# A of the fourth pair of heads for the first four batches by 11 block products, placed between the two halves of U

## Chip, cores and metric

The kernel runs on one core of a Trainium2 chip. The metric is the device time of one execution in microseconds (us). The engines are PE (TensorE, matrix products; PEld is its loading of weights), DVE (VectorE), ACT (ScalarE), POOL (GpSimd) and SP (SyncE, which only issues DMAs here). Each works its own instructions in the order of the program, and waits on semaphores for the others.

## Reference

Cross-attention with 8 heads of 256, all in float32: x is 16 x 256 x 256 (batch, queries, width), c is 16 x 77 x 192.

```python
Q = (x @ Wq).reshape(B, -1, H, D).transpose(0, 2, 1, 3)
K = (c @ Wk).reshape(B, -1, H, D).transpose(0, 2, 1, 3)
V = (c @ Wv).reshape(B, -1, H, D).transpose(0, 2, 1, 3)
score = jnp.einsum('bhqd,bhkd->bhqk', Q, K) / math.sqrt(D)   # masked keys: -inf
attn = softmax(score)
ctx = jnp.einsum('bhqk,bhkd->bqhd', attn, V).reshape(B, -1, H * D)
out = ctx @ Wo + x
return layernorm(out) * gamma + beta
```

## Kernel before

The kernel folds weights. Per head, G = Wk Wq^T / 16 (192 x 256) is made once, so that the scores are x (G^T c^T); the product A = G^T c^T (256 x 77 for a head and batch) takes the place of K and Q. Likewise U = Wv Wo per head takes the place of V and the output projection. The batches go in four groups of four (GB = 4); a row tile is 128 queries, two for a batch, 32 in all.

G is kept in gA (its first 128 rows, for all 8 heads) and gB (its last 64 rows, two heads of a pair above each other); c, turned, in cA and cB in the same split. U is kept in uA and uB.

A is made in one of two ways.

- Straight: `prepare_a`, whose products into the banks pa are lines L203 (with gA) and L215 (with gB). The first group's A is made so, one pair of heads at a time (`a_of_pairs`).
- By 11 block products in place of 12: `prepare_fast`, in the manner of Strassen and Winograd. It takes one pair of heads of a group, and treats batches 0-1 and 2-3 of the group and the halves of G as 2 x 2 blocks. `products()` issues 44 matrix products (line L361) into four PSUM banks pf, a middle and an end bank for each head; ACT copies one product of each head out on the way (L370); `put_together(e)` adds a head's blocks up into A with four operations of DVE (L373). The operands are sums and differences of blocks: of G in gS (`sums_of_g`, `last_sums_of_g`) with a copy gC, of c in cT and cD (`sums_of_c`, `differences_of_c`), all made by POOL after copies of ACT. Groups 1 and 2 of four use it; t_of and cD are indexed by the group less one.

The lines of the start, in the program's order:

1. Loads. SP issues them all in one queue; a load waits for the eighth before it to land. POOL issues every second block of Wv (wvT) in its own queue.
2. Wk and Wq of a pair are turned (`turn_blk`, DVE) into kT and qT; then gB's products (phb, L1033), gA's (pgb, L1017), and A of the pair (pa). Pair 0 goes by other lines. kT lies in a room with the tag gS; after the last pair the same room is given to the sums of G.
3. Wv is turned (`turn_v`, DVE, L945).
4. U, in two halves j of two pairs each: `of_pair` into banks pu (L956), copies into uA; `rest_of_pairs` into banks pw (L970), copies into uB.
5. Scores of the first two row tiles (ps, L469), masking and maxima on DVE (`shift`, L486), exponentials on ACT (L512), weights p on POOL (`weigh`, L533), turned on DVE (`turn`, L543).
6. `prepare_last` (pr, L429 and L440), U times c for two batches (pv, L393 and L404), A of group 1 by `prepare_fast` for two pairs (pf), and so on in steps of two batches.

PSUM has eight banks, given out in turn: a tile waits until the reader of the tile eight banks before it is done. With it, the scores of row tile 2 take the banks of pf's first pair, and the scores of row tile 4 the last two banks of pf's second pair.

The order on each engine is the order of the code (`manual_schedule`).

Of the kernel before, what the change touches and what calls it, by code (L numbers as in the profile page):

```python
# [9 lines left out]
F32 = mybir.dt.float32  # L10
# [6 lines left out]
P = 128  # L17
H = 8
# [9 lines left out]
def kernel(  # L28
# [13 lines left out]
    nc = tc.nc  # L42
# [45 lines left out]
    cT = const.tile([P, 4, FAST, KX], F32, tag="cT", name="cT")  # L88
    cD = const.tile([P, FAST, KX], F32, tag="cD", name="cD")
    gC = const.tile([P, NF, P], F32, tag="gC", name="gC")  # L90

    def flat(ap):
        return ap.rearrange("p a b -> p (a b)")
# [34 lines left out]
    def half(i):  # L128
        return slice(i * LB, (i + 1) * LB)
# [99 lines left out]
        partial(nc.gpsimd.tensor_tensor, op=op) for op in (ALU.add, ALU.subtract)  # L229
    )  # L230

    def parts_of_g():
        parts = gA.rearrange("p (u e) (dc i c) -> p dc e u i c", e=2, dc=2, c=BK)
        sums = gS.rearrange("p n (u e) (i c) -> p n e u i c", e=2, c=BK)
        return [(parts, sums, e, own, other) for e, own, other in ((0, high, low), (1, low, high))]

    def sums_of_g():


        for parts, sums, e, own, other in parts_of_g():  # L240
            nc.scalar.copy(sums[own, 0, e], parts[other, 1, e])
            nc.scalar.copy(gC[own], gB[other, :, P:])
        for parts, sums, e, own, other in parts_of_g():
            s1, s2, s3 = (sums[own, n, e] for n in range(3))
            add(s1, s1, parts[own, 1, e])
            subtract(s2, s1, parts[own, 0, e])
            subtract(s3, parts[own, 0, e], parts[own, 1, e])

    def last_sums_of_g():


        for parts, sums, e, own, other in parts_of_g():
            nc.scalar.copy(sums[other, 0, e], sums[own, 1, e])
        for parts, sums, e, own, other in parts_of_g():
            subtract(sums[other, 0, e], parts[other, 0, e], sums[other, 0, e])

    def halves_of(c, lo, hi):
        groups = c[:, lo * GB : hi * GB].rearrange("p (g y b) k -> p y g (b k)", y=2, b=HB)
        return groups[:, 0], groups[:, 1]

    def sums_of_c(lo, hi):


        xs, ys = halves_of(cA, lo, hi)
        t1, t2, t3, t4 = (cT[:, n, lo - 1 : hi - 1] for n in range(4))
        subtract(t1, ys, xs)
        for own, other in ((low, high), (high, low)):
            nc.gpsimd.tensor_copy(t2[own], ys[other])
        subtract(t3, t2, ys)
        subtract(t2, t2, t1)  # L270
        for own, other in ((low, high), (high, low)):
            nc.gpsimd.tensor_copy(t4[own], t2[other])
        subtract(t4, xs, t4)

    def differences_of_c(lo, hi):
        subtract(cD[:, lo - 1 : hi - 1], *halves_of(cB, lo, hi))

    def prepare_fast(g, u):

# [19 lines left out]
            return lambda i: gA[rows, h, dc * P + i * LB : dc * P + (i + 1) * LB]  # L299

        def from_s(rows, n, h):
            return lambda i: gS[rows, n, h, half(i)]

        def from_rest(h, dc):
            return lambda i: gB[half(h % 2), h // 2, dc * P + i * LB : dc * P + (i + 1) * LB]
# [2 lines left out]
            return flat(of[rows, which])  # L308

        def t_of(rows, n):  # L310
            return cT[rows, n, g - 1]

        def middle(e):

# [13 lines left out]
        def outer(e):  # L328

            h, own = heads[e], (low, high)[e]  # L330
            return [
                ((ends[e], 0), from_g(own, h, 0), c_of(cA, own, xs)),
                ((ends[e], 1), from_s(own, 0, h), c_of(cA, own, ys)),
                ((ends[e], 2), from_g(own, h, 1), t_of(own, 3)),
                ((ends[e], 0), from_rest(h, 0), c_of(cB, own, xs)),
                ((ends[e], 1), from_rest(h, 0), c_of(cB, own, ys)),
                ((ends[e], 2), from_rest(h, 1), cD[own, g - 1]),
            ]

        def pairs():  # L340
# [442 lines left out]
    with tc.tile_pool(name="wonce", bufs=1) as wp:  # L783
# [15 lines left out]
        def load_blocks(to, blocks, queues=(nc.sync,)):  # L799
            for i in range(NM):  # L800
                queues[i % len(queues)].dma_start(to[i * BK : (i + 1) * BK], blocks[i])
# [35 lines left out]
            return parts[::-1] if a == 1 else parts  # L837

        qT_blk = [const.tile([P, 4, DI], F32, tag=f"xg{a}", name=f"qT_{a}") for a in range(NF)]
        kT_all = const.tile([P, NF, 4, DL], F32, tag="gS", name="kT_all")  # L840
        kT_blk = [kT_all[:, a] for a in range(NF)]
        qT = qT_blk[0].rearrange("p (e dc) d -> p e dc d", e=2)
        kT = kT_blk[0].rearrange("p (e dc) l -> p e dc l", e=2)
        for a in range(1, NF):
# [21 lines left out]

        def load_late():

            for a in range(NF):
                load_blocks(wvT[a], wv_blocks[a], (nc.sync, nc.gpsimd))  # L870
            for a in range(NF):
                nc.sync.dma_start(wo_of[a // 2][:, a % 2], wo_rows[a])
            load_xT(0, QT)
            load_bias(0, GB)
            load_rest()
            load_xT(QT, PT)
            load_xT(PT, GT)
            load_bias(GB, B)
# [65 lines left out]
        def turn_v(a):  # L944
            nc.vector.transpose(  # L945
                wv_turned[:, a].rearrange("p n (r m) -> p m n r", r=BK),
                wvT[a].rearrange("p m (c n) -> p m n c", n=4),
            )
# [112 lines left out]
        turn_k_last()  # L1061
        g_of(1)
        turn_c()
        load_late()
        rest_of_g()
        turn_blk(1)
        a_of_pairs(0)
        for a in range(1, NF):
            rest_of_g_of_pair(a)
            g_of_pair(a)  # L1070
            if a < NF - 1:
                turn_blk(a + 1)
            else:
                for i in range(3):
                    turn_v(i)
            a_of_pairs(a, rest_first=True)
        gS = const.tile([P, 3, H, P], F32, tag="gS", name="gS")
        sums_of_g()
        load_x(0)
        load_x(1)  # L1080
        nc.sync.dma_start(gam, gamma.partition_broadcast(P))
        nc.sync.dma_start(bet, beta.partition_broadcast(P))
        turn_v(3)

        def sum_of(u):
            t2, _, b22, b11, b12 = (u[:, q].rearrange("p n i c -> p (n i c)") for q in range(5))
# [3 lines left out]
        for j in range(NF // 2):  # L1090
            pu = two_banks("pu", j)
            for a in range(2 * j, 2 * j + 2):
                of_pair(pu, a, wv_part, wo_part)
            if j:
                transpose_x(0)
                bias_of(0, GB)
            for e, copy in enumerate((nc.scalar.copy, nc.scalar.copy if j else nc.vector.tensor_copy)):
                copy(
                    of_e(uA, e)[:, :, 2 * j : 2 * j + 2].rearrange("p n a c -> p a n c"),
                    pu[e].rearrange("p a (n c) -> p a n c", c=BK),  # L1100
                )
            if j:
                sum_of(uA)
            for e, pw in enumerate(
                rest_of_pairs(j, (2 * j, 2 * j + 1), wv_part, wo_part, "pw")
            ):
                copy = (nc.scalar.copy, nc.vector.tensor_copy)[e]
                for i in range(2):
                    for k in range(2):
                        copy(  # L1110
                            of_e(uB, e)[half(k), :, 2 * j + i],
                            pw[half(i)].rearrange("p (n c) -> p n c", c=BK),
                        )
        last_sums_of_g()
        for t in range(QT):
            scores(t)
        turn_rest()
# [291 lines left out]
```

## Time and profile before

| | |
|---|---|
| median of 3 runs | 269.1 us (268.92 to 269.33) |
| the profiled execution | 268.58 us |
| its span in the profile | 266.8 us |
| PE, PEld | 260.5 us (98%), 202.8 us (76%) |
| DVE, ACT, POOL | 212.7 us (80%), 166.9 us (63%), 191.5 us (72%) |
| granted clock of PE | 1.0 in the span's mean |

The span is the time between the first and the last instruction of the trace. Busy time is what each engine worked in it. A row of the chain gives its start, its length and what it is; "x32" counts records, and a float32 product has two. A row of a timeline gives start, busy time, engine, line, operation, output<-input with partitions x elements, and in brackets how long the engine stood idle ahead of it, and what ended that.

### The profile page before, as it was taken

Reading aid. Unit: us, or ns where it says so; the run is one execution under the profiler, and the core shown is the slowest. Engines: PE = TensorE matmul, PEld = TensorE weight load, DVE = VectorE, ACT = ScalarE, POOL = GpSimd, SP = SyncE. Lnnn points to the kernel's source line nnn. Section 1 sums busy time; section 2 is a strip of 40 time slices with the busy share of each in tenths; the row PEclk is TensorE's granted clock in tenths of the full one; section 3 lists DMA queues with packets and bytes.
Section 4 is the critical chain, followed back from the end, with each engine's and each line's share of the span. In section 5 each row is a group of like instructions: output and inputs, shape, how many; then the busy total and the mean of one; then the engine's idle time right before and its main releaser. Section 6 shows DMA issues by size and latency. Waiting matters only on the chain.

```text
span 266.8 us, 15067 instructions
## 1 busy us (share of the span) xinstructions
PE 260.5 (98%) x6330; PEld 202.8 (76%) x6330; DVE 212.7 (80%) x860; ACT 166.9 (63%) x710; POOL 191.5 (72%) x272
## 2 busy tenths in 40 slices
PE   7999999999999999999999999999999999999992
PEld 6566578948986899679967996799669957985662
DVE  0554968479893789988997969898988798799785
ACT  3253548624584689648983798467964595636772
POOL 1042098799459896899479996997699899685452
PEclk9999999999999999999999999999999999999999
DMA  6999997900240002131314012221234010100112
GB/s 188 209 206 225 335 148 160 300 18 4 63 104 5 2 6 66 58 90 37 83 43 122 5 24 65 81 85 41 54 127 132 20 44 2 44 23 25 42 43 80
DMA packets 41699, 22.73 MB, mean 85 GB/s; under 512 B 24144, under 2 KB 40608, under 8 KB 41632
## 3 DMA queue, kind: packets, MB, share of 16 engines
q1 hardware_dynamic: 41248, 20.98, 31.3%
q0 software_dynamic: 384, 0.79, 1.3%
q8 instruction: 50, 0.82, 1.3%
q14 instruction: 17, 0.14, 0.2%
HBM read 17.57 MB, written 4.19 MB: 82 GB/s over the span
## 4 chain that ended last, share of the span: by engine, by line
PE 96%; DMA 2%; DVE 1%; SPq 0%; issue 0%; DVEq 0%
PE ps L469 25%; PE pf L361 11%; PE po L622 11%; PE pv L393 10%; PE pm L622 9%; PE pv L404 6%; PE pa L203 5%; PE po L555 4%; PE pu L956 3%; PE pa L215 2%; PE pr L429 2%; PE pgb L1017 2%; DMA wq_nat<-in_L_xattn_Wq_dram 2%; PE pw L970 1%; PE pr L440 1%; PE phb L1033 1%
## 5 line engine op out<-in xcount | busy, mean ns | idle before, releaser
L512 ACT ACTIVATE s<-s,top 128x77 f32<-128x77 f32 x256 | 85.2, 346 | 24.5 <-DVE top L486 24.5
L469 PE MATMUL ps<-a,xT 128*32 128x154 f32 x2048 | 70.1, 294 | 0.0
L469 PEld LDWEIGHTS ps<-a,xT 128*32 128x32 f32 x2048 | 65.8, 110 | 2.0 <-issue 1.5
L533 POOL TENSOR_TENSOR p<-s,rden 128x512 f32<-128x512 f32 x64 | 47.7, 769 | 21.9 <-DVE rden L527 21.7
L486 DVE CUSTOM_DVE_ANT_0 s<-ps,bias 128x77 f32<-128x77 f32 x256 | 43.3, 232 | 4.6 <-PE ps L469 4.0
L512 ACT ACTIVATION_READ_ACCUMULATOR s<-s,top 128x1 f32 x224 | 41.9, 187 | 0.0
L373 DVE TENSOR_TENSOR a<-pf,a 128x154 f32<-128x154 f32 x80 | 33.9, 435 | 7.3 <-PE pf L361 4.9
L664 POOL TENSOR_TENSOR xg<-xg,m 128x256 f32<-128x256 f32 x39 | 28.8, 738 | 2.7 <-DVE xg L676 0.7
L543 DVE STREAM_TRANSPOSE pT<-p 128x640 f32<-128x640 f32 x32 | 26.3, 827 | 5.1 <-POOL p L533 5.0
L393 PE MATMUL pv<-uA,cA 128*32 128x512 f32 x256 | 29.6, 593 | 0.0
L1150 ACT COPY vw<-pv 128x512 f32<-128x512 f32 x32 | 17.1, 587 | 14.9 <-PE pv L404 14.9
L760 DVE SCALAR_TENSOR_TENSOR xg<-xg,rstd,bet 128x256 f32<-128x256 f32 x27 | 22.7, 840 | 2.6 <-ACT rstd L711 1.2
L586 POOL TENSOR_TENSOR ts<-vw 128x768 f32<-128x768 f32 x13 | 23.6, 1831 | 0.0
L486 DVE DVE_READ_ACCUMULATOR2_ANT top<- 128x1 f32 x256 | 20.9, 82 | 0.0
L393 PEld LDWEIGHTS pv<-uA,cA 128*32 128x32 f32 x256 | 8.0, 110 | 13.3 <-issue 9.8
L731 DVE SCALAR_TENSOR_TENSOR xg<-xg,mv,gam 128x256 f32<-128x256 f32 x30 | 18.0, 600 | 0.1
L361 PE MATMUL pf<-cT,gS 64*64 64x154 f32 x240 | 17.4, 290 | 0.0
L603 POOL TENSOR_TENSOR ss<-pT 128x256 f32<-128x256 f32 x13 | 9.7, 745 | 9.8 <-DVE pT L543 9.7
L404 PE MATMUL pv<-uB,cB 64*32 64x512 f32 x256 | 16.3, 596 | 0.0
L622 PE MATMUL po<-vr,pT 128*32 128x256 f32 x208 | 16.0, 379 | 0.0
L361 PEld LDWEIGHTS pf<-cT,gS 64*64 64x64 f32 x240 | 15.8, 133 | 0.0
L203 PE MATMUL pa<-cA,gA 128*32 128x308 f32 (+1 forms) x256 | 14.0, 360 | 0.0
(153 smaller groups left out, 543.1 us busy)
## 6 DMA issues: line engine op xcount, KB each, us to landing
xg<-in_x_dram SPq DMA_DIRECT2D x8, 512.0 KB, 4.4
xT<-in_x_dram SPq DMA_DIRECT2D x56, 64.0 KB, 2.7
out_dram<-xg SPq DMA_DIRECT2D x11, 256.0 KB, 2.7
wo<-in_L_xattn_Wo_dram SPq DMA_DIRECT2D x4, 512.0 KB, 7.9
wq_blk<-in_L_xattn_Wq_dram SPq DMA_DIRECT2D x12, 128.0 KB, 4.6
out_dram<-xg SPq DMA_DIRECT2D x10, 128.0 KB, 1.7
wk_blk<-in_L_xattn_Wk_dram SPq DMA_DIRECT2D x12, 96.0 KB, 4.0
wvT<-in_L_xattn_Wv_dram POOLq DMA_DIRECT2D x8, 96.0 KB, 6.3
```

Of the source, the lines that this page charges most:

```text
L203: nc.tensor.matmul(flat(o[i * BK : (i + 1) * BK]), gA[:, h, cols(dc, i)], flat(cA[:, batches, :]), start=not rest_first and n in opening, ...
L361: nc.tensor.matmul(bank[half(i), n], weight(i), moving, start=start, stop=stop,)
L373: nc.vector.tensor_tensor(out, *of, ALU.add)
L393: nc.tensor.matmul(pv[k][i * BK : (i + 1) * BK], cA[:, b, k * BK : (k + 1) * BK], uA[:, parts, :, i], start=not rest_first, stop=rest_first,)
L404: nc.tensor.matmul(pv[k][i * BK : (i + 1) * BK], cB[half(k), b, k * BK : (k + 1) * BK], uB[half(k), parts, :, i], start=rest_first, stop=n ...
L469: nc.tensor.matmul(ps[m // 2][i * BK : (i + 1) * BK, m % 2 * 2 * S2 : (m % 2 + 1) * 2 * S2], xT_of[t // PT][:, j * NM + m, dc], flat(a_of[ ...
L486: nc.vector.tensor_tensor_reduce(s[:, h], ps[a][:, k * S2 : (k + 1) * S2], bias[:, b, :], scale=-1.0, scalar=FAR, op0=ALU.add, op1=ALU.min ...
L512: nc.scalar.activation(s[:, h], s[:, h], AF.Exp, bias=top[:, one], scale=-1.0, accum_out=den[:, one] if summed_by_act(t) else None,)
L533: nc.gpsimd.tensor_tensor(part, e_mh[:, :, :, keys], rden_mh.unsqueeze(3).to_broadcast(list(part.shape)), ALU.mult,)
L543: nc.vector.transpose(pT_of[t].rearrange("p n m q -> p m n q"), p.rearrange("p m (n k) -> p m n k", k=BK),)
L622: nc.tensor.matmul(out[i * BK : (i + 1) * BK], weight[:, i], moving, start=first and n == 0, stop=final and n == len(terms) - 1,)
L664: nc.gpsimd.tensor_tensor(to, to, what, ALU.add)
```

## The change

A of the fourth pair of heads (a = 3, heads 6 and 7) of the first group is no longer made straight, right behind its G, but by `prepare_fast(0, 3)`, in the loop over the halves of U, behind the first half's products. For that:

- sums and differences of c of the first group are made right behind `turn_c`, on POOL, in the places of cT and cD that group 3 takes later (`places_of`, and `(g - 1) % FAST`);
- the sums of G are made by pairs. gS becomes one tile of 4 x 3 x 2 x 128 per partition, which holds a pair's turned Wk until that pair's G is made, and then its sums. The fourth pair's sums come first (`sums_of_g(3, 4)`, `last_sums_of_g(3, 4)`), behind its G; those of the other three come behind the first half of U;
- Wv's turns: the first goes ahead of the fourth pair's gB copies, the second behind them, the last two into the first half of U, where `transpose_x(0)` goes too;
- the copies of the first half of U out of pu and pw are all ACT's (before, DVE copied one of the two pu banks and one of the two pw banks);
- the loads of Wv and Wo are interleaved by halves.

```diff
+    gS = const.tile([P, NF, 3, 2, P], F32, tag="gS", name="gS")
...
-    def parts_of_g():
+    def parts_of_g(lo, hi):
         parts = gA.rearrange("p (u e) (dc i c) -> p dc e u i c", e=2, dc=2, c=BK)
-        sums = gS.rearrange("p n (u e) (i c) -> p n e u i c", e=2, c=BK)
-        return [(parts, sums, e, own, other) for e, own, other in ((0, high, low), (1, low, high))]
...
+        sums = gS.rearrange("p u n e (i c) -> p n e u i c", c=BK)
+        return [
+            (parts[:, :, :, lo:hi], sums[:, :, :, lo:hi], e, own, other)
+            for e, own, other in ((0, high, low), (1, low, high))
+        ]
...
+    def places_of(lo, hi):
+        return slice((lo - 1) % FAST, (hi - 2) % FAST + 1)
...
-        t1, t2, t3, t4 = (cT[:, n, lo - 1 : hi - 1] for n in range(4))
+        t1, t2, t3, t4 = (cT[:, n, places_of(lo, hi)] for n in range(4))
...
-            return cT[rows, n, g - 1]
+            return cT[rows, n, (g - 1) % FAST]
...
-            for a in range(NF):
-                load_blocks(wvT[a], wv_blocks[a], (nc.sync, nc.gpsimd))
-            for a in range(NF):
-                nc.sync.dma_start(wo_of[a // 2][:, a % 2], wo_rows[a])
+            for j in range(NF // 2):
+                for a in range(2 * j, 2 * j + 2):
+                    load_blocks(wvT[a], wv_blocks[a], (nc.sync, nc.gpsimd))
+                for a in range(2 * j, 2 * j + 2):
+                    nc.sync.dma_start(wo_of[j][:, a % 2], wo_rows[a])
...
         turn_c()
+        sums_of_c(0, 1)
+        differences_of_c(0, 1)
...
             if a < NF - 1:
                 turn_blk(a + 1)
-            else:
-                for i in range(3):
-                    turn_v(i)
-            a_of_pairs(a, rest_first=True)
-        gS = const.tile([P, 3, H, P], F32, tag="gS", name="gS")
-        sums_of_g()
+                if a == NF - 2:
+                    turn_v(0)
+                a_of_pairs(a, rest_first=True)
+        turn_v(1)
+        sums_of_g(NF - 1, NF)
+        last_sums_of_g(NF - 1, NF)
...
-        turn_v(3)
...
             if j:
-                transpose_x(0)
                 bias_of(0, GB)
-            for e, copy in enumerate((nc.scalar.copy, nc.scalar.copy if j else nc.vector.tensor_copy)):
-                copy(
+            for e in range(2):
+                nc.scalar.copy(
...
-            for e, pw in enumerate(
-                rest_of_pairs(j, (2 * j, 2 * j + 1), wv_part, wo_part, "pw")
-            ):
-                copy = (nc.scalar.copy, nc.vector.tensor_copy)[e]
+            rests = rest_of_pairs(j, (2 * j, 2 * j + 1), wv_part, wo_part, "pw")
+            if j == 0:
+                products, put_together = prepare_fast(0, NF - 1)
+                products()
+            for e, pw in enumerate(rests):
+                copy = nc.vector.tensor_copy if j and e else nc.scalar.copy
...
+            if j == 0:
+                for i in range(2, NF):
+                    turn_v(i)
+                transpose_x(0)
+                for e in range(2):
+                    put_together(e)
+                sums_of_g(0, NF - 1)
-        last_sums_of_g()
+        last_sums_of_g(0, NF - 1)
```

**POOL**, from the sums of G (gS) to the last two of them, before (nan and bias belong to the mask, uA is half of U):

```order
L245 TENSOR_TENSOR gS<-gS,gA 64x4x128
L246 TENSOR_TENSOR gS<-gS,gA 64x4x128
L247 TENSOR_TENSOR gS<-gA 64x4x128
L245 TENSOR_TENSOR gS<-gS,gA 64x4x128
L246 TENSOR_TENSOR gS<-gS,gA 64x4x128
L247 TENSOR_TENSOR gS<-gA 64x4x128
L777 TENSOR_TENSOR nan_634<-nan_634 128x4
L778 TENSOR_TENSOR nan_634<-nan_634 128x4
L779 TENSOR_TENSOR bias<-bias,nan_634 128x308
L1087 TENSOR_TENSOR uA<-uA 128x512
L1088 TENSOR_TENSOR uA<-uA 128x512
L255 TENSOR_TENSOR gS<-gA,gS 64x4x128 x2
```

POOL now, from the first sums of the three pairs on (ahead of these rows stand the fourth pair's eight, on 64x128):

```order
L249 TENSOR_TENSOR gS<-gS,gA 64x3x128
L250 TENSOR_TENSOR gS<-gS,gA 64x3x128
L251 TENSOR_TENSOR gS<-gA 64x3x128
L249 TENSOR_TENSOR gS<-gS,gA 64x3x128
L250 TENSOR_TENSOR gS<-gS,gA 64x3x128
L251 TENSOR_TENSOR gS<-gA 64x3x128
L784 TENSOR_TENSOR nan_682<-nan_682 128x4
L785 TENSOR_TENSOR nan_682<-nan_682 128x4
L786 TENSOR_TENSOR bias<-bias,nan_682 128x308
L1095 TENSOR_TENSOR uA<-uA 128x512
L1096 TENSOR_TENSOR uA<-uA 128x512
L259 TENSOR_TENSOR gS<-gA,gS 64x3x128 x2
```

The mask and U stood behind six operations on four pairs (64x4x128); now they stand behind eight on one pair and six on three pairs (64x3x128).

**ACT**, from the last copy of A to the second half of U, before (gC is the copy of gB, uA and uB are U):

```order
L1055 COPY a_256<-pa_7_1_0_489 128x4x77
L241 COPY gS<-gA 64x4x128
L242 COPY gC<-gB 64x512
L241 COPY gS<-gA 64x4x128
L242 COPY gC<-gB 64x512
L1098 COPY uA<-pu_0_536 128x2x8x32
L1110 COPY uB<-pw_0_572 64x8x32 x4
L1098 COPY uA<-pu_0_598 128x2x8x32
L1098 COPY uA<-pu_1_599 128x2x8x32
L1110 COPY uB<-pw_0_643 64x8x32 x4
```

ACT now, from the copies for the fourth pair's last sums on:

```order
L257 COPY gS<-gS 64x128 x2
L1105 COPY uA<-pu_0_514 128x2x8x32
L1105 COPY uA<-pu_1_515 128x2x8x32
L377 COPY a_265<-pf_6_0_568 128x2x77
L377 COPY a_265<-pf_7_1_570 128x2x77
L1119 COPY uB<-pw_0_550 64x8x32 x4
L1119 COPY uB<-pw_1_551 64x8x32 x4
L245 COPY gS<-gA 64x3x128
L246 COPY gC<-gB 64x384
L245 COPY gS<-gA 64x3x128
L246 COPY gC<-gB 64x384
L1105 COPY uA<-pu_0_647 128x2x8x32
```

The copies that start the sums of G (L241, now L245) stood ahead of all copies of U; those of three pairs now stand behind the first half of U, behind two copies of pf and behind eight copies of pw.

**SP**, the loads of Wv (wvT) and Wo, before:

```order
L801 DMA wvT_145<-in_L_xattn_Wv_dram 32x6x128 x2
L801 DMA wvT_146<-in_L_xattn_Wv_dram 32x6x128 x2
L801 DMA wvT_147<-in_L_xattn_Wv_dram 32x6x128 x2
L801 DMA wvT_148<-in_L_xattn_Wv_dram 32x6x128 x2
L872 DMA wo_143<-in_L_xattn_Wo_dram 128x1024 x2
L872 DMA wo_144<-in_L_xattn_Wo_dram 128x1024 x2
```

And now:

```order
L808 DMA wvT_145<-in_L_xattn_Wv_dram 32x6x128 x2
L808 DMA wvT_146<-in_L_xattn_Wv_dram 32x6x128 x2
L879 DMA wo_143<-in_L_xattn_Wo_dram 128x1024 x2
L808 DMA wvT_147<-in_L_xattn_Wv_dram 32x6x128 x2
L808 DMA wvT_148<-in_L_xattn_Wv_dram 32x6x128 x2
L879 DMA wo_144<-in_L_xattn_Wo_dram 128x1024 x2
```

Wo's first half moved ahead of the second half of Wv.

More of the change, by code (lines that the diff above doesn't have):

```diff
@@ L230, with sums_of_g @@
     )
-    def parts_of_g():
+    def parts_of_g(lo, hi):
         parts = gA.rearrange("p (u e) (dc i c) -> p dc e u i c", e=2, dc=2, c=BK)
-        sums = gS.rearrange("p n (u e) (i c) -> p n e u i c", e=2, c=BK)
-        return [(parts, sums, e, own, other) for e, own, other in ((0, high, low), (1, low, high))]
-    def sums_of_g():
-        for parts, sums, e, own, other in parts_of_g():
+        sums = gS.rearrange("p u n e (i c) -> p n e u i c", c=BK)
[3 more added lines that the diff above has]
+        ]
+    def sums_of_g(lo, hi):
+        for parts, sums, e, own, other in parts_of_g(lo, hi):
             nc.scalar.copy(sums[own, 0, e], parts[other, 1, e])
-            nc.scalar.copy(gC[own], gB[other, :, P:])
-        for parts, sums, e, own, other in parts_of_g():
+            nc.scalar.copy(gC[own, lo:hi], gB[other, lo:hi, P:])
+        for parts, sums, e, own, other in parts_of_g(lo, hi):
             s1, s2, s3 = (sums[own, n, e] for n in range(3))
@@ L247, in sums_of_g, with last_sums_of_g @@
             subtract(s3, parts[own, 0, e], parts[own, 1, e])
-    def last_sums_of_g():
-        for parts, sums, e, own, other in parts_of_g():
+    def last_sums_of_g(lo, hi):
+        for parts, sums, e, own, other in parts_of_g(lo, hi):
             nc.scalar.copy(sums[other, 0, e], sums[own, 1, e])
-        for parts, sums, e, own, other in parts_of_g():
+        for parts, sums, e, own, other in parts_of_g(lo, hi):
             subtract(sums[other, 0, e], parts[other, 0, e], sums[other, 0, e])
@@ L275, in differences_of_c @@
     def differences_of_c(lo, hi):
-        subtract(cD[:, lo - 1 : hi - 1], *halves_of(cB, lo, hi))
+        subtract(cD[:, places_of(lo, hi)], *halves_of(cB, lo, hi))
     def prepare_fast(g, u):
@@ L301, in from_s @@
         def from_s(rows, n, h):
-            return lambda i: gS[rows, n, h, half(i)]
+            return lambda i: gS[rows, u, n, h % 2, half(i)]
         def from_rest(h, dc):
@@ L336, in outer @@
                 ((ends[e], 1), from_rest(h, 0), c_of(cB, own, ys)),
-                ((ends[e], 2), from_rest(h, 1), cD[own, g - 1]),
+                ((ends[e], 2), from_rest(h, 1), cD[own, (g - 1) % FAST]),
             ]
@@ L839 @@
         qT_blk = [const.tile([P, 4, DI], F32, tag=f"xg{a}", name=f"qT_{a}") for a in range(NF)]
-        kT_all = const.tile([P, NF, 4, DL], F32, tag="gS", name="kT_all")
-        kT_blk = [kT_all[:, a] for a in range(NF)]
+        kT_blk = [gS[:, a].rearrange("p n e c -> p (n e c)").rearrange("p (n l) -> p n l", n=4) for a in range(NF)]
         qT = qT_blk[0].rearrange("p (e dc) d -> p e dc d", e=2)
```

## Prediction

> **What bounds the kernel now.** I read the page first, then the chain of waits between 0 and 85 us, then the timelines of POOL, ACT and DVE between 20 and 80 us, last the landing of the weight loads. The page:
>
> ```profile
> span 266.8 us, 15067 instructions
> PE 260.5 (98%) x6330; PEld 202.8 (76%) x6330; DVE 212.7 (80%) x860; ACT 166.9 (63%) x710; POOL 191.5 (72%) x272
> PE 96%; DMA 2%; DVE 1%; SPq 0%; issue 0%; DVEq 0%
> ```
>
> PE is the chain: 96% of it. After the first 7 us PE stands idle nowhere, so each microsecond of products removed is a microsecond gained, and each new wait of PE is lost for good. The place of the change, in the chain (start, us, what):
>
> ```profile
> 26.56 1.73 PE pgb L1017 x32
> 28.29 1.04 PE pa L215 x16
> 29.32 2.21 PE pa L203 x32
> 31.53 3.62 PE pu L956 x64
> 35.15 1.73 PE pw L970 x32
> 36.87 3.45 PE pu L956 x64
> ...
> 52.20 3.01 PE pr L440 x32
> ...
> 60.66 5.93 PE pf L361 x176
> 66.59 4.32 PE ps L469 x128
> ...
> 74.83 4.19 PE ps L469 x128
> ```
>
> The two pa rows at 28.29 and 29.32 are A of the fourth pair, which the change takes out. The pf row is two pairs done by the 11 block products (A of batches 4 to 7), which is the row that prices what is put in. The next rows are of POOL, whose work is what can make PE wait later (start, us busy, in brackets the idle time before and what ended it):
>
> ```profile
> 17.16 4.67 POOL L801 DMA_DIRECT2D wvT<-in_L_xattn_Wv_dram  x8 [6.56 <-DMA wk_blk<-in_L_xattn_Wk_dram]
> 32.80 1.29 POOL L245 TENSOR_TENSOR gS<-gS,gA 64x512 f32<-64x512 f32 x1 [10.97 <-ACT gS L241]
> 39.31 1.26 POOL L247 TENSOR_TENSOR gS<-gA 64x512 f32<-64x512 f32 x1
> 41.34 0.20 POOL L777 TENSOR_TENSOR nan<-nan 128x4 f32<-128x4 f32 x1 [0.77 <-DVE nan L776]
> 45.16 2.63 POOL L255 TENSOR_TENSOR gS<-gA,gS 64x512 f32<-64x512 f32 x2
> 48.88 0.93 POOL L823 COPY cB<-cB 64x896 f32<-64x896 f32 x1 [1.09 <-DVE cB L822]
> 49.86 0.36 POOL L824 COPY last_rows<-cB 128x208 f32<-128x208 f32 x1
> 56.29 2.72 POOL L533 TENSOR_TENSOR p<-s,rden 128x512 f32<-128x512 f32 x4
> 58.97 1.00 POOL L276 TENSOR_TENSOR cD<-cB 128x462 f32<-128x462 f32 x1
> 60.03 0.74 POOL L603 TENSOR_TENSOR ss<-pT 128x256 f32<-128x256 f32 x1
> ```
>
> Between 32.80 and 59.97 POOL has only two gaps, 0.77 and 1.09 us, and from 48.88 none. What waits for its end is DVE:
>
> ```profile
> 27.89 6.20 DVE L945 STREAM_TRANSPOSE wv_turned<-wvT 128x768 f32<-128x768 f32 x4
> 59.05 0.85 DVE L543 STREAM_TRANSPOSE pT<-p 128x640 f32<-128x640 f32 x1 [0.49 <-POOL p L533]
> 63.83 5.46 DVE L373 TENSOR_TENSOR a<-pf,a 128x154 f32<-128x154 f32 x12
> 72.43 0.20 DVE L527 RECIPROCAL rden<-den 128x8 f32<-128x8 f32 x1 [0.62 <-ACT s L512]
> 72.55 1.80 DVE L373 TENSOR_TENSOR a<-pf,a 128x154 f32<-128x154 f32 x4
> ```
>
> p of tile 1 leaves POOL at 59.01 (56.29 + 2.72) and DVE starts on it at 59.05; from there it runs without a gap until the put-together rows at 63.83. These free the PSUM banks of pf. PE's scores of tile 2, at 66.59, take the banks of pf's first head, free after four of the twelve operations, at 63.83 + 5.46 x 4/12 = 65.65: 0.94 us to spare. Its scores of tile 4, at 74.83, take the banks of pf's last head, free at 72.55 + 1.80 = 74.35: 0.48 us to spare. So POOL's order is already within half a microsecond of PE's chain.
>
> **The change, part by part.**
>
> *Products.* Out go 1.04 + 2.21, that is 28.29 to 31.53, 3.24 us; in come 44 products, half of the pf row: 2.97 us. All of it is on the chain: -0.27 us.
>
> *U starts earlier.* pu's first product now follows pgb, at 28.29 and not 31.53. It needs the first turned Wv, the first half of Wo and the second Wv 1.73 us later. The turns take 6.20/4 = 1.55 us each; the first goes ahead of gB's copies, into DVE's idle time; the second starts at 27.89 as the first does now, and ends by 29.5, ahead of 30.0. The loads:
>
> ```profile
> L801 SPq DMA_DIRECT2D wvT<-in_L_xattn_Wv_dram x2: 602/602/602, 19.8 to 20.5; - x2
> DMA to landing us min/median/max: 6.7/6.8/6.9
> L801 POOL DMA_DIRECT2D wvT<-in_L_xattn_Wv_dram x1: 567/567/567, 21.3 to 21.3; - x1
> DMA to landing us min/median/max: 7.3/7.3/7.3
> L872 SPq DMA_DIRECT2D wo<-in_L_xattn_Wo_dram x1: 592/592/592, 23.9 to 23.9; - x1
> DMA to landing us min/median/max: 7.1/7.1/7.1
> ```
>
> SP's second-tile Wv load issued at 19.8 lands at 26.5 and the third tile's, at 20.5, at 27.4; Wo's first load takes that place now. Before, Wo landed at 31.0, 3.6 us after the 27.4 of that third tile, with three more Wv loads of SP's queue ahead of it, about 0.9 us apiece by the spacing 26.5 to 27.4; it took some 0.9 to 1.1 us itself. So 26.5 + 1.1 = 27.6 is the low end, no wait; if POOL's own queue, whose last Wv load lands at 21.3 + 7.3 = 28.6, goes wholly first, 29.7, a wait of 1.4 us. The two queues' loads land side by side, so I stay near the low end: 0.1 us.
>
> *Sums of the first group of c.* Seven small operations and a difference on POOL, put behind turn_c: today the same seven and uB's two sums lie between 50.22 (49.86 + 0.36) and 56.29, and two sums of that size take 2.63 (L255), so the seven take 3.4 us, and the difference of 154 columns under 0.74 (a row of 256). POOL's idle 6.56 us before 17.16 covers them. Cost 0; without that cover the Wv loads of POOL's queue would be late.
>
> *Sums of G for the fourth pair.* Eight operations on 128 columns, about 0.47 us each by the line through 256 and 512 columns (0.74 and 1.27), on POOL from about 29.3 (pgb's end at 28.29, then ACT's two copies of gA and one of gS) to about 33.1: idle there today (10.97). The new pf starts at 28.29 + 0.1 + 3.62 + 1.73 = 33.74: 0.6 us to spare, cost 0.
>
> *Sums of G for the other three pairs.* This is what costs. ACT prepares them, and its row now reads: two copies of the new pf, eight copies of pw (four were DVE's), then the copies for the sums.
>
> ```profile
> 32.04 0.62 ACT L241 COPY gS<-gA 64x512 f32<-64x512 f32 x1
> 36.92 1.50 ACT L1110 COPY uB<-pw 64x256 f32<-64x256 f32 x4 [1.14 <-PE pw L970]
> 45.05 0.37 ACT L819 COPY last_rows<-cA 128x208 f32<-128x208 f32 x1 [0.17 <-DVE cA L818]
> 61.66 0.29 ACT L370 COPY a<-pf 128x154 f32<-128x154 f32 x1 [0.22 <-PE pf L361]
> ```
>
> The second copy of pf ends 61.66 + 0.29 - 60.66 = 1.29 us behind pf's start, the eight take 3.00, the copy of 384 columns lies between 0.37 (208) and 0.62 (512): 0.51; POOL starts 0.14 behind it (32.04 + 0.62 to 32.80). So POOL starts 4.94 us behind pf, at 38.68, where today three of its six operations are done. One operation on 384 columns lies midway between 256 columns, 0.74, and 512, 1.27: 1.00 us. The six took 7.77 (32.80 to 40.57), now 7.77 x 1.00/1.27 = 6.12, to 44.80. The mask's three and uA's two follow, as between 41.34 and 45.16, 3.82, and the last two sums, 2.63 x 1.00/1.27 = 2.07. POOL comes to cB's copy at 38.68 + 6.12 + 3.82 + 2.07 = 50.69, and not 48.88: **1.81 us late**, both its gaps being used up.
>
> From there nothing on POOL gives way, so p of tile 1, DVE's chain behind it and the banks come 1.81 us late: the banks for tile 4 at 74.35 + 1.81 = 76.16, where PE started at 74.83. PE starts that much later: **+1.33 us** against before, the 0.27 won included. (At tile 2 the same reckoning gives 65.65 + 1.81 - 66.59 = +0.87, the first part of it.) Behind it DVE waits for PE again, and the lateness stays.
>
> The Trainium skill, GPSIMD Engine Reference, Elementwise — side-by-side cycle accounting, gives about 2.6 cycles an element at 1.2 GHz for such a two-input operation: 0.83 us for 384 columns (an estimate from that page), with which the sum would come to about -0.1 us. By that rule 512 columns would be 1.11, where this trace has 1.27: it agrees in the slope (256 to 512 columns: 2.07 ns each) but leaves out a part of 0.2 us.
>
> *Other moves.* DVE gets eight put-together operations (3.6 us) and loses four copies of pw and one of uA; they end near 41, ahead of pw's end at about 41.9, behind which the scores read them. The mask's sum on POOL comes 3.46 us later (44.80 against 41.34); the masking of tile 0 then waits for it some 1 us, which brings the banks that pr's last products want just in time. cRB is copied at 50.22 + 1.81 = 52.03, just when PE's L440 row (52.20 - 0.17) wants it: 0 to 0.1 us, and absorbed in the later wait. xg, gamma and beta load for work far behind. Cost 0.
>
> Sum: the profiled execution took 268.58 us (span 266.8 and 1.8 around it), 0.5 below the median 269.1 of the runs; 268.58 + 1.33 = 269.9, on the median's scale **270.4 us**, 0.5% slower.
>
> **Rivals.**
>
> *The cover holds.* POOL's wide operations are cheaper than midway, or ACT reaches the sums sooner, so that POOL is less than 0.31 us late (0.48 spare less the 0.17 that PE is early). It needs operations of about 0.81 us on 384 columns. Then only the products count: 269.1 - 0.27 + 0.1 = 268.9, no change to be measured; with more luck in pu's start (3.62 the first time against 3.45 the second) 268.7. For it: a page's rule, above. Against it: every POOL row of this size. This is the case that ends not slower; 20%.
>
> *Wo late.* If the loads of POOL's queue go first, pu waits up to 1.4 us, and all that follows with it: 270.4 + 1.3 = 271.7. For it: Wo lands today 0.5 us before its use. Against: the two queues are served side by side. 12%.
>
> *Lateness partly made up.* If DVE or ACT save time between 59 and 74 us, only tile 2's wait is left, or less: +0.3 to +0.9, 269.4 to 270.0. Within my forecast's own range.
>
> **How the numbers follow.** The forecast (a POOL order that comes 1 to 2.3 us late, 269.6 to 270.9) 62%, the cover holds 20%, Wo late 12%, something unseen 6%. The range reaches from the cover that holds, 268.9, to part of Wo's wait, 271.3. A measurement of this kernel can tell about 0.2%, 0.54 us, from no change. Slower: 52 of the forecast's 62, Wo's 12, 1: 65%. Same: 10 and 13 of the cover's 20, 1: 24%. Faster: 11%.
>
> **What would show it.** In the chain after: pgb followed at once by pu near 28.3, one pf row of x88 and 2.97 us near 33.7; ACT's copies of pw eight in a row; POOL's first 64x384 operation near 38.7 at 1.00 us and cB's copy near 50.7 with no idle before it; DVE's turn of p's second tile near 60.9 behind POOL; PE idle before the scores of tiles 2 and 4, released by DVE a, about 1 and 0.5 us. Wrong, if 64x384 takes 0.85 or less, if cB's copy still waits for DVE, or if PE waits at pu for Wo.

## The result: 0.7% slower, by loads and not by POOL

| | before | after |
|---|---|---|
| median of the runs | 269.1 us (268.92 to 269.34, 6 runs) | 271.17 us (270.41 to 271.58, 6 runs) |
| ratio after / before | | 1.0072, 95% interval 1.0057 to 1.0087 |
| the profiled execution, its span | 268.58 us, 266.8 us | 271.23 us, 269.2 us |

The forecast was 270.4, in a range of 268.9 to 271.3, with the sign right; the middle of that range (269.6 to 270.9) was missed. The profile after says that the sign came about in another way, and one of the prediction's own signs of being wrong is there: PE waits at pu for Wo. The page's shares of the chain, and the chain itself from the start of U on:

```profile
PE 86%; DMA 7%; SPq 4%; DVE 1%; issue 1%; DVEq 0%
```

```profile
21.45 10.73 DMA wo<-in_L_xattn_Wo_dram
32.31 1.96 PE pu L963 x32
34.27 1.73 PE pw L977 x32
36.00 2.88 PE pf L368 x88
38.88 3.45 PE pu L963 x64
42.33 1.73 PE pw L977 x32
44.06 4.33 PE ps L476 x128
...
68.59 0.14 issue
68.74 4.39 PE ps L476 x128
...
77.05 4.23 PE ps L476 x128
```

Where the chain was 96% PE, 11% of it is now loads and their issue (2% before). It leaves PE at the second load of Wo. PE's own timeline and its waits show how long it stood:

```profile
26.80 1.91 PE L1024 MATMUL pgb<-qT,gS 64*64 64x256 f32 x32
29.91 1.96 PE L963 MATMUL pu<-wo,wv_turned 64*64 64x256 f32 x32 [1.20 <-DVE wv_turned L952]
32.31 1.96 PE L963 MATMUL pu<-wo,wv_turned 64*64 64x256 f32 x32 [0.45 <-DMA wo<-in_L_xattn_Wo_dram]
```

Wo's loads, by the view of their tile (issue times at the end of the first row):

```profile
L879 SPq DMA_DIRECT2D wo<-in_L_xattn_Wo_dram x2: 592/1154/1717, 20.8 to 21.4; - x2
DMA to landing us min/median/max: 9.0/9.8/10.7
```

They were asked for 3.1 and 3.3 us sooner than before (23.9 and 24.7), and landed at 29.8 and 32.2, where they had landed at 31.0 and 32.2. DVE's turns of Wv and of x's first tiles:

```profile
24.81 1.67 DVE L952 STREAM_TRANSPOSE wv_turned<-wvT 128x768 f32<-128x768 f32 x1 [0.40 <-DMA wvT<-in_L_xattn_Wv_dram]
...
28.28 1.59 DVE L952 STREAM_TRANSPOSE wv_turned<-wvT 128x768 f32<-128x768 f32 x1
...
38.89 0.71 DVE L176 STREAM_TRANSPOSE xT<-xT 128x512 f32<-128x512 f32 x1 [2.60 <-DMA xT<-in_x_dram]
39.63 3.70 DVE L380 TENSOR_TENSOR a<-pf,a 128x154 f32<-128x154 f32 x8
...
67.45 5.45 DVE L380 TENSOR_TENSOR a<-pf,a 128x154 f32<-128x154 f32 x12
...
76.18 1.80 DVE L380 TENSOR_TENSOR a<-pf,a 128x154 f32<-128x154 f32 x4
```

The first wait is put down to DVE, whose second turn of Wv ends at 29.87 (28.28 + 1.59); but these first products read the first turn, done at 26.48, and Wo's first load, landed at 29.8. A releaser is inferred from what came last, and here two things came together. The profile of e2 (below) tells them apart: there PE starts on pu before the second turn is done, at 29.98 (28.38 + 1.60), and right behind Wo's load, issued at 20.98 and landed 8.4 us later:

```profile
29.48 1.96 PE L963 MATMUL pu<-wo,wv_turned 64*64 64x256 f32 x32 [0.66 <-DMA wo<-in_L_xattn_Wo_dram]
```

```profile
28.38 1.60 DVE L952 STREAM_TRANSPOSE wv_turned<-wvT 128x768 f32<-128x768 f32 x1
```

From the last pgb on (its start differs by 0.42 us between the two profiles, and that start is as late in a run of the kernel before that differs only behind it, b1 below), the account is:

- U's first half: 5.56 us (from pgb's end, 26.80 + 1.91 = 28.71, to 34.27) for 3.62: **+1.94**. Of it 1.65 are the two waits; the rest is that two rows which stand apart take 2 x 1.96 us, where 64 products in one go took 3.62.
- the new products: 2.88 for 3.24: **-0.36**, as forecast (-0.27).
- from the first scores to those of tile 4: 32.99 us for 32.78: **+0.21**, all of it at tile 2 (0.14 ahead of that row, 0.07 in it). The forecast had +1.50 here: it let the first scores start 0.17 us early and those of tile 4 1.33 us late.

1.94 - 0.36 + 0.21 is 1.79, and with the 0.42 ahead of it 2.21 of the 2.4 us between the spans. 0.18 more lies behind tile 4.

POOL is late much as forecast:

```profile
40.52 1.00 POOL L249 TENSOR_TENSOR gS<-gS,gA 64x384 f32<-64x384 f32 x1 [6.81 <-ACT gS L245]
...
52.55 0.93 POOL L830 COPY cB<-cB 64x896 f32<-64x896 f32 x1
...
59.98 2.71 POOL L540 TENSOR_TENSOR p<-s,rden 128x512 f32<-128x512 f32 x4
```

1.00 us an operation, no idle time before cB's copy, p 3.69 us later than before: 1.68 later than the first scores, which are 2.01 later (forecast: 1.81). DVE follows it (its last rows above), and yet PE hardly waits.

PE's scores of tile 2 do wait for DVE, by 0.14 us. They start at 68.74, 1.29 us behind the first of DVE's twelve operations (67.45). In all five profiles in which PE stands ahead of these scores (after, b1, f1, e7, f4) they start 1.27 to 1.29 us behind it; in the others 2.07 us or more, and PE does not stand. The rows are the waits of PE's sequencer (PEldq) ahead of the scores, the longest of them 0.81 us and for DVE's semaphore, and DVE's second and third operation, done at 68.63:

```profile
L476 PEldq EVENT_SEMAPHORE  x3: 51/51/814, 67.6 to 67.9; - x3
```

```profile
67.80 0.83 DVE L380 TENSOR_TENSOR a<-pf,a 128x308 f32<-128x308 f32 x2
```

In the kernel, the first three operations of a head read its middle bank, the fourth its end bank, and the first scores of tile 2 take the place of the middle bank. So the wait is for the bank that the forecast named, but it is free after three operations, 1.29 us behind the first, and not after four, 1.82. Before, PE had 66.59 - 63.83 - 1.29 = 1.47 us to spare there, and not 0.94. DVE's row comes 3.62 us later than before and the first scores 2.01, so DVE is 1.61 us later against PE: 0.14 more than the 1.47.

The scores of tile 4 start at 77.05, while the last four operations still run, up to 77.98. So they do not wait for these, and what stands ahead of the prediction on the banks of tile 4, with its 0.48 us to spare, does not fit the trace. Which bank they take was not found out.

### The profile page after: what moved, and what is told of

Its sections match the earlier page's. It is cut to its first block, busy times and chain, and to the rows that moved or that the text cites. A ratio compares the mean times of both kernels' runs of the same rounds, so it can differ in the third digit from the quotient of the medians.

```text
span 269.2 us, 15180 instructions
## 1 busy us (share of the span) xinstructions
PE 261.0 (97%) x6370; PEld 205.9 (77%) x6370; DVE 212.3 (79%) x863; ACT 168.6 (63%) x719; POOL 196.3 (73%) x289
## 3 DMA queue, kind: packets, MB, share of 16 engines
q1 hardware_dynamic: 41248, 20.98, 31.3%
## 4 chain that ended last, share of the span: by engine, by line
PE 86%; DMA 7%; SPq 4%; DVE 1%; issue 1%; DVEq 0%
PE ps L476 25%; PE pf L368 12%; PE po L629 10%; PE pv L400 10%; PE pm L629 8%; PE pv L411 6%; PE po L562 4%; DMA wo<-in_L_xattn_Wo_dram 4%; SPq L808 2%; PE pr L436 2%; PE pu L963 2%; DMA wk_blk<-in_L_xattn_Wk_dram 2%; PE pa L204 2%; DMA wq_blk<-in_L_xattn_Wq_dram 1%; PE pw L977 1%; PE pr L447 1%
## 5 line engine op out<-in xcount | busy, mean ns | idle before, releaser
L380 DVE TENSOR_TENSOR a<-pf,a 128x154 f32<-128x154 f32 x88 | 37.3, 435 | 7.7 <-PE pf L368 4.9
L368 PE MATMUL pf<-cT,gS 64*64 64x154 f32 x264 | 19.1, 290 | 0.0
L368 PEld LDWEIGHTS pf<-cT,gS 64*64 64x64 f32 x264 | 17.4, 133 | 0.0
L368 PE MATMUL pf<-cB,gB 64*64 64x154 f32 x176 | 15.4, 290 | 0.0
```

The costliest lines, as they stand in the source:

```text
L368: nc.tensor.matmul(bank[half(i), n], weight(i), moving, start=start, stop=stop,)
L380: nc.vector.tensor_tensor(out, *of, ALU.add)
```

## Experiments

Ratios are to the kernel before, timed in turn with the runs of that row's group: its median was 269.1 us with e1, e2, e3 and b1, 268.93 with e4, e7, e8 and e10, and 268.89 with f1 to f4. In brackets stands the 95% interval.

| run | median us | ratio (95%) | first scores behind the last pgb, us |
|---|---|---|---|
| before | 269.1 | | 15.67 |
| after | 271.17 | 1.0072 (1.0057 to 1.0087) | 17.26 |
| e1: no wait for Wo | 270.11 | 1.0037 (1.0023 to 1.0051) | 16.65 |
| e2: POOL light | 270.30 | 1.0052 (1.0033 to 1.0071) | 16.70 |
| e3: both | 270.03 | 1.0036 (1.0018 to 1.0055) | 16.35 |
| b1: before, POOL late | 269.21 | 1.0010 (0.9994 to 1.0026) | 15.67 |
| e4: Wv's second half by SP | 270.39 | 1.0063 (1.0033 to 1.0094) | 16.85 |
| f1: A together first | 270.94 | 1.0070 (1.0044 to 1.0096) | 16.46 |
| e7: e4 and f1 | 269.41 | 1.0016 (1.0007 to 1.0025) | 15.52 |
| e8: e7, sums early | 269.27 | 1.0016 (1.0002 to 1.0029) | 15.92 |
| f3: e8, gB by ACT | 269.03 | 1.0011 (0.9999 to 1.0023) | 15.20 |
| f2: e8, no wait for Wo | 269.10 | 1.0013 (0.9999 to 1.0026) | 16.19 |
| e10: Wv's second half by SP and ACT | 272.23 | 1.0123 (1.0100 to 1.0146) | 18.27 |
| f4: loads in the order of before | 273.02 | 1.0134 (1.0105 to 1.0162) | 19.79 |

The last column is from each run's one profile (start of the scores of tile 0 in the chain, less the start of the third pgb row in PE's timeline), so it varies with that execution's loads.

**Is it POOL?** b1 puts the forecast's cause alone into the kernel before; e2 takes it out of after.

```diff
-            subtract(sums[other, 0, e], parts[other, 0, e], sums[other, 0, e])   # b1, in last_sums_of_g
+            for _ in range(1 if e else 3):
+                subtract(sums[other, 0, e], parts[other, 0, e], sums[other, 0, e])
```

> The kernel before, with one of the last two sums of G made three times (64x512, 1.3 us each), so that POOL comes to the copy of cB 2.63 - 1.09 = 1.5 us late, as in the change measured against PE, with nothing else changed. Theory POOL: PE starts the scores of tile 4 1.54 - 0.48 = 1.06 us later: 270.2 us. Theory Wo: PE needs the banks of pf's first head later than the forecast took it to, so 0 to 0.3 us: 269.1 to 269.4.

The chain of b1, and its p on POOL:

```profile
27.14 1.73 PE pgb L1018 x32
...
67.33 4.39 PE ps L470 x128
...
75.64 4.19 PE ps L470 x128
```

```profile
58.53 2.71 POOL L534 TENSOR_TENSOR p<-s,rden 128x512 f32<-128x512 f32 x4
```

pgb starts 0.58 us later in this execution than in that of before, with no edit ahead of it. Less that, p is 58.53 - 56.29 - 0.58 = 1.66 us late, the same as in after; the scores of tile 2 are 0.16 late, those of tile 4 0.23, the time +0.1 us within its interval. The forecast's step asked for +1.06, which lies outside that interval. It is refuted.

```diff
-            (parts[:, :, :, lo:hi], sums[:, :, :, lo:hi], e, own, other)   # e2; few is 1 for the sums
+            (parts[:, :, :, lo:hi, :few], sums[:, :, :, lo:hi, :few], e, own, other)   # of the three pairs
```

> The changed kernel, but the sums of G of the three pairs are made on a quarter of their columns only (96 in place of 384), so that POOL comes to the copy of cB about 4 us sooner, not late any more; the rest of gS is left as it was, so the later A are others. Theory Wo: only the small waits behind 68 us go, about 0.3 us: 270.8. Theory POOL: the late sums are most of the loss, 1.3 us: 269.8 us.

Without POOL's lateness the ratio is 1.0052, and its interval overlaps that of after; 270.30 lies midway between the two times expected, so it decides nothing by itself. In its profile the first scores and those of tile 4 are 32.78 us apart (43.61 to 76.39), as before: the 0.21 is what POOL's lateness cost. PE still waits 1.1 us for Wo.

**Is it Wo?**

```diff
-            return wo_of[a // 2][half(e), a % 2, n, :]   # e1, e3 (with e2's edit), f2 (with e8's)
+            return gA[half(e), n, :] if a < 2 else wo_of[a // 2][half(e), a % 2, n, :]
```

> The changed kernel, but the first half of U takes columns of G (gA, ready at 17 us) in the place of Wo's first two rows, whose loads are still made: PE's wait for Wo is gone, all else stays, U's values are others. Theory Wo: the changed kernel loses 1.2 + 0.45 us by PE waiting for Wo at the start of U; pu follows pgb at once, 271.17 - 1.65 = 269.5 us. Theory POOL (the forecast's step: POOL's late sums cost PE 1.3 us at the scores of tiles 2 and 4, and POOL's start hangs on pf, so it comes earlier with it): 270.4 us, the forecast without its 0.1 of Wo, and PE waits of about 1 us stand at those scores.

> Both edits: gA in the place of Wo's first two rows, and the three pairs' sums on a quarter of their columns. Theory Wo: 271.17 - 1.65 - 0.3 = 269.2, and what is left is the gain of the products, so about 268.8 to 269.2. Theory POOL: 269.0, the two parts adding up the other way round (1.3 by POOL, 0.7 by Wo).

Half of the loss goes, not all of it: e1's 270.11 lies between the two times expected (269.5 and 270.4), e3's 270.03 above both of its own (269.2 and 269.0). PE's waits in e1, and DVE's rows ahead of the first scores:

```profile
PE ps L476 <- DVE a L380: 0.9, 1, 0.9
```

```profile
38.98 0.71 DVE L176 STREAM_TRANSPOSE xT<-xT 128x512 f32<-128x512 f32 x1 [1.77 <-DMA xT<-in_x_dram]
39.73 3.69 DVE L380 TENSOR_TENSOR a<-pf,a 128x154 f32<-128x154 f32 x8
```

Behind Wo's wait stood a second one, hidden by it: DVE turns x's first tiles, whose load lands at 38.9, and only then puts A together, to 43.4; the scores of tile 0 need both. In after DVE's rows are the same (38.89, 39.63 + 3.70 = 43.33), with PE at 44.06 just behind. e3 has no wait for Wo either; its profile shows 0.8 us in pw for which no releaser is named, and I did not find its cause.

**Two limits, one behind the other.** Each has a cure that leaves nothing out.

```diff
-                    load_blocks(wvT[a], wv_blocks[a], (nc.sync, nc.gpsimd))      # e4
+                    load_blocks(wvT[a], wv_blocks[a], (nc.sync,) if j else (nc.sync, nc.gpsimd))
```

```diff
-                transpose_x(0)      # f1
                 for e in range(2):
                     put_together(e)
+                transpose_x(0)
```

> After, with the second half of Wv loaded by SP's queue alone, in its place behind Wo's first half; nothing is left out. POOL's queue then carries only the first half's four blocks. Theory now (U's first product waits 1.2 us and its second pair 0.4 us for Wo's two loads, which share the DMA engines with POOL's blocks of Wv's second half; 4 x 96 KB at the 210 to 250 GB/s of the trace are 1.6 us of transfer taken from ahead of Wo): Wo's first load lands 1 to 1.6 us sooner, PE's wait at pu falls from 1.6 us to 0.5 or less, and the time falls, but not by all of it, since the run without Wo's wait showed the first scores held to 43.5 us by x's load and DVE's putting together: 269.9 to 270.4. Rival (the loads together are bound by the sum of bytes, whichever queue carries them, and Wo does not land sooner): 271.2, as after. Rival of the prediction (POOL late): 271.2 less nothing that a load order changes, 271.0 to 271.3.

> After, with the fourth pair's A put together by DVE ahead of its turn of x's first tiles, and nothing else; nothing is left out. This edit gained 1.0 us where Wv's second half had been moved to SP. Theory now (two limits one behind the other: U's wait for Wo holds the first scores to 44.06 us, where x and the putting together would let them go at 43.4): by itself it gains nothing much, 270.8 to 271.4. Rival (the order on DVE costs 1 us by itself, whatever the loads do): 270.2.

> As the run before it (second half of Wv by SP alone), and DVE puts the fourth pair's A together ahead of its turn of x's first tiles, not behind it; nothing is left out. Theory (behind Wo's wait, the next thing that the first scores wait for is x's late load, at 38.9 us, with 3.7 us of DVE's putting together behind it): the scores of tile 0 start 0.7 to 1.0 us sooner than without this edit, near 42.5 us, and the time comes to 269.2 to 269.7. Rival (what is left is POOL's lateness): no gain over the run before it, 269.9 to 270.4. Rival (run to run scatter of the loads at the start makes up the rest): also no gain over the run before it.

Alone, either does next to nothing: 1.0063 and 1.0070, against 1.0072. Together they give 1.0016. e4's profile has no wait at pu, and one of 1.2 us at the first scores; f1's has 1.0 at pu and none there. e7's chain has neither:

```profile
28.84 1.73 PE pu L963 x32
...
30.63 1.96 PE pu L963 x32
32.58 1.73 PE pw L977 x32
...
42.46 4.32 PE ps L476 x128
```

Wo lands sooner in e4 because less is ahead of it: its two loads took 7.4 and 9.0 us in place of 9.0 and 10.7, with the four blocks of Wv that POOL's queue had carried beside them now behind.

```profile
DMA to landing us min/median/max: 7.4/8.2/9.0
```

This is no accident of one profile: over the five with the load order of after (after, e1, e2, e3, f1) the two loads took 8.4 to 9.9 and 9.7 to 11.3 us, over the five with that of e4 (e4, e7, e8, f2, f3) 6.1 to 7.7 and 7.6 to 9.5. e4's median is in the range that I gave, but its spread is wide (269.06 to 272.37), and by the ratio its gain is less than I expected.

**What is left.** e8 makes the three pairs' sums as soon as their G is there; f3 also lets ACT copy the fourth pair's gB, so that DVE goes straight from one turn of Wv to the next.

```diff
                 if a == NF - 2:      # e8, beside e7's edits
                     turn_v(0)
+                    sums_of_g(0, NF - 1)
...
-                sums_of_g(0, NF - 1)
```

```diff
-                    nc.vector.tensor_scalar(...)   # f3, pair 3 of rest_of_g_of_pair
...
+        for dst, src in between() if between else ():   # in sums_of_g(3, 4), between its copies to gS and to gC
+            nc.scalar.mul(dst, src, D ** -0.5)
```

> As the run before it, and the sums of G of the first three pairs made as soon as their G is there (near 25 us, POOL idle) in place of behind the new products (40.5 us); nothing is left out. This takes POOL's lateness away without leaving work out. Theory now (POOL's lateness cost PE 0.1 to 0.3 us, not 1.06): 0 to 0.3 us under the run before it, 269.0 to 269.5. Prediction's step (POOL's lateness costs PE 1.33 - 0.27 = about 1.06 us at the scores of tiles 2 and 4): 1 us under the run before it.

> The version with all three cures, and the four copies of the fourth pair's gB made by ACT (behind its copies for the fourth pair's sums) in place of DVE, so that DVE goes from one turn of Wv to the next; nothing is left out. Theory (what is left is a wait for Wv's late turns in some executions, 0.3 us at U's second pair in the profiled one): 0.1 to 0.3 us under the version with all three cures, 268.8 to 269.2. Rival (the wait is for Wo or the landing of Wv itself): no change, 269.2 to 269.4; if ACT's four copies hold up gC, up to 0.5 us slower.

> The version with all three cures (second half of Wv by SP, A put together first, sums of three pairs early), and U's first half reads G in Wo's place: the first half of U is left wrong by that, and none of its products wait for Wo. It shows what the change is worth with no wait for Wo at all. Theory (the products save 0.27 to 0.36 us of PE, and nothing else of the change costs): 268.5 to 268.9, so 0.1 to 0.4 us under before. Rival (something else in the change costs about 0.3 us, since the version with all three cures is still 0.3 us over before): 269.1 to 269.4.

With POOL not late any more (in e8's profile it waits 1.52 us for DVE ahead of cB's copy), the time moved by 0.14 us, within its scatter: what 1.7 us of lateness costs is 0.1 to 0.2, as in b1 and e2. e8's profile waits 0.3 us at pu for a turn of Wv, f2's 0.8, though f2 has no wait for Wo. f3's profile has no such wait:

```profile
28.26 3.45 PE pu L966 x64
31.71 1.73 PE pw L980 x32
33.44 2.93 PE pf L371 x88
36.37 3.45 PE pu L966 x64
39.82 1.73 PE pw L980 x32
41.55 4.32 PE ps L479 x128
...
66.08 4.32 PE ps L479 x128
...
74.33 4.19 PE ps L479 x128
```

This is the change as the products alone would have it: every row from 28.26 without a gap, and the scores of tiles 0, 2 and 4 each 0.5 us earlier than before (42.05, 66.59, 74.83). That execution took 268.57 us with a span of 266.5, that of before 268.58 with 266.8. But in twelve executions f3 went from 268.57 to 269.96 where before stays in 268.47 to 269.73: a median of 269.03 against 268.89. It is 0.6% better than after, and not to be told from before. Taking Wo's wait out altogether gains no more: f2's 269.10 is its rival's number and not its theory's. In f2's profile Wv's landing takes the place of Wo's, and in f3's, where nothing waits, the products save what they should. That the landing of Wv is what costs in the other executions too is likely, but not shown.

**Whose loads?** Two more orders, both worse.

```diff
-                    load_blocks(wvT[a], wv_blocks[a], (nc.sync, nc.gpsimd))   # e10, beside f1's and e8's edits;
+                    load_blocks(wvT[a], wv_blocks[a], (nc.sync, None) if j else (nc.sync, nc.gpsimd))
...
+                    for v in range(2, NF):                                # POOL's share is ACT's, behind pair 2's G
+                        load_blocks(wvT[v], wv_blocks[v], (None, nc.scalar))
```

> After, with all three cures, but the second half of Wv shared by SP and ACT: ACT issues its four blocks behind its copies of the third pair's G (near 25 us), so that they start behind Wo's first half as well; A put together ahead of x's turn, sums of three pairs early. Nothing is left out. If the order of transfers is all that matters: Wo's first half lands before 28.5 us, no wait at pu, scores of tile 0 near 42.0, and the time is that of before less the 0.3 us of products: 268.8 to 269.3. If SP's longer queue is no limit, the same as the run before it within 0.3 us. If ACT's issues (about 0.6 us each) hold up A of the third pair: up to 1 us slower than the run before it.

None of the three: 272.23. SP's row of e10 and PE's waits:

```profile
19.11 6.79 SPq L809 DMA_DIRECT2D wvT<-in_L_xattn_Wv_dram  x4
25.94 1.07 SPq L880 DMA_DIRECT2D wo<-in_L_xattn_Wo_dram  x2
```

```profile
PE pu L964 <- DMA wo<-in_L_xattn_Wo_dram: 2.7, 2, 2.3
```

SP's fourth load of Wv stood until 25.3, when the first of ACT's (issued at 22.69) had landed, by the chain. So Wo was asked for 5 us later than in after. In the trace the two loads use one and the same landing semaphore, and a load waits for the eighth before it; that ACT's loads count among the eight would explain the stop, but it was not tried.

```diff
-            for j in range(NF // 2):         # f4: the lines of before, all of Wv and then all of Wo
...
+            for a in range(NF):
+                load_blocks(wvT[a], wv_blocks[a], (nc.sync, nc.gpsimd))
+            for a in range(NF):
+                nc.sync.dma_start(wo_of[a // 2][:, a % 2], wo_rows[a])
```

> After, with the loads of Wv and Wo in the order of before (all of Wv, then all of Wo); nothing is left out. Theory (the DMA engines are busy without a gap up to about 36 us, and what U's first half needs last, Wo's second load, landed at 32.2 us in both orders): U's first product waits longer, to about 31.0, the second pair follows without a wait, and the first half ends at 34.5 in place of 34.3: 271.1 to 271.6, no different from after. Rival (the interleaved order is what lets U start early, by the 1.2 us by which Wo's first load lands sooner): 272.2 or more.

273.02, and so the rival's number; but the landings were the theory's: 24.2 + 6.7 = 30.9, and the second about 32.1. PE started at 30.96, as expected, and took 5.37 us for U's half, though nothing is named as late. The clock tells (columns: stretch, its length, busy time of PE, PEld, DVE, ACT, POOL, granted clock, DMA share, GB/s):

```profile
32.00:33.00 1.00, 1.00 (x20) 0.83 (x15) 0.30 (x1) 0.22 (x1) 0.93 (x3) 0.63 1.21 255
33.00:34.00 1.00, 1.00 (x13) 0.69 (x11) 0.00 (x0) 0.00 (x0) 0.25 (x1) 0.50 1.20 180
34.00:35.00 1.00, 1.00 (x16) 0.79 (x12) 0.00 (x0) 0.00 (x0) 0.00 (x0) 0.50 0.96 160
35.00:36.00 1.00, 1.00 (x20) 0.76 (x16) 0.00 (x0) 0.00 (x0) 0.00 (x0) 0.66 0.32 59
```

After 2.72 us without a product PE ran four microseconds at a mean clock of 0.57: 4 x 0.43 = 1.7 us lost, about the 1.8 us between the 34.5 expected and 36.33. So f4's median hardly speaks for the rival: four of its six executions, with mean granted clocks of 0.991 to 0.994, took 272.9 to 273.38 us; the two others, with 0.998 and 0.999, took 270.76 and 271.93, on either side of the theory's 271.1 to 271.6.

## Why the prediction was right in sign, and where it failed

- *Products, -0.27.* Right: -0.36, and -0.3 to -0.5 us in f3's profile, where nothing else waits.
- *U's start, 0.1 us.* **This is the first step that failed: 1.94 us came out.** "The two queues' loads land side by side, so I stay near the low end" took Wo's own time, 0.9 to 1.1 us, from the spacing of landings in SP's queue, where 96 KB blocks land. Wo's loads are 512 KB each: at the 213 to 279 GB/s of the first two rows below, 1.9 to 2.5 us apiece (an estimate from these rows), and in after the two landed 2.4 us apart. And the DMA engines were busy all along: their share, the last column but one, is

```profile
20.00:22.00 2.00, 2.00 (x56) 1.68 (x59) 0.88 (x4) 0.42 (x1) 2.00 (x5) 1.00 1.10 213
28.00:30.00 2.00, 0.80 (x20) 0.31 (x16) 1.84 (x2) 1.17 (x5) 0.10 (x1) 1.00 1.02 279
34.00:36.00 2.00, 2.00 (x48) 1.69 (x43) 2.00 (x2) 1.07 (x2) 0.00 (x0) 1.00 1.21 238
```

  about 1 up to 36 us (before, up to 34). The share tells that the engines were busy, not that no more bytes would fit: at about 1 the rate went from 208 to 336 GB/s in the stretches of after. But Wo's first load, asked for 3.1 us sooner, landed only 1.2 us sooner, and e4 shows that blocks put behind it bring it forward. The waits of 1.65 us are past the bounds that I had set (0 to 1.4). What the rival "Wo late" (271.7, at 12%) said of Wo happened, without the 1.33 us of POOL that its number holds, and without its condition: of POOL's loads, two landed behind Wo's first.
- *POOL late.* The order, 1.00 us an operation, a cB copy without idle time, 1.68 us late: all right. *What waits for it* is **the second step that failed**: +0.21 in place of +1.50. The 0.94 and 0.48 us to spare rested on whole heads of pf being free. The traces show PE starting on tile 2 after three operations of DVE and not four, which leaves 1.47 us, and on tile 4 before the last four have ended. b1 shows that 1.66 us of lateness costs 0.1 to 0.2. So what the rival "the cover holds" said of POOL's cost came out, but not for its reason: an operation took 1.00 us and not 0.81.
- *DVE's put-together, cost 0, "they end near 41".* They end at 43.33, behind x's load, which I had not followed. Hidden by Wo's wait in after, it is what held e1 and e4.
- *A cover that was thin.* With U 3 us sooner, Wv's first turn waits for its load (24.0 to 26.6 us over these profiles), where before DVE came to it at 27.89. This I did not price; it may be why the versions with the change spread more widely than before, which was not tried.

That the number came near is luck: U's start was put 1.84 us too low (0.1 for 1.94) and the wait for POOL 1.29 us too high (1.50 for 0.21), and the two partly cancelled.

## To carry to other kernels

Before moving work earlier, look at the DMA share of the stretch from which its operands come: where it is about 1, as here, name the bytes that are to land later for these to land sooner. Where removing a wait gains little, look for a second one just behind it: of two limits in series, either cure alone shows nothing (here 1.0063 and 1.0070 against 1.0072, and 1.0016 for both). Slack in front of a PSUM bank is to be counted from the last operation that reads that one bank (here the third of four), and checked against when PE in the trace actually started.

## What the hardware showed beyond that

A gap of PE can cost more than its length: 2.72 us without products in f4 were followed by a granted clock of 0.63, 0.50, 0.50 and 0.66 in four successive microseconds. In the profiles of after and e10, gaps of 1.20 and 0.45 us and of 2.33 us left it at 1.00. The Trainium skill, TensorE: Matmul & The Clock Gate, Part 1: The HAM clock gate, says that the clock halves behind an idle window of about 3.4 us that runs freely. The half rate agrees (0.50); the gap that was enough here is shorter than that window. That it matters where the gap falls in the window is not shown here.

The mean granted clock of every execution is on record. It is 0.993 or less in eight, which took 272.73 to 273.38 us: three each of f4 and e10, one each of f1 and e2. So the longest execution of f1 (272.79, at 0.993) goes with such a drop; the longest of e4 (272.37, at 0.998) does not, and its wide spread stays open.
